# Layer 1's output projection, layer norm and ternary feed forward as one pipeline of four stages over token tiles

## The chip, the cores and the metric

The program runs on one core of one Trainium2 chip. The core has a matrix engine (TensorE, PE in the profile, with its weight loads shown apart as PEld), VectorE (DVE), ScalarE (ACT), GpSimd (POOL) and SyncE (SP), which here only issues DMAs. Each engine takes its instructions in the order in which they were laid down; engines wait for each other by semaphores. Matrix products land in PSUM, everything else lives in the on-chip memory SBUF or in the device memory behind the DMA queues. The metric is the device time of one execution in microseconds (us), lower being better.

## The reference, cut to what matters

The program is a decoder of four layers on x of 8 x 100 tokens and 512 features. Each layer adds a cross attention on a context of 8 x 361 rows and then a feed forward, both of a layer-normed x. The change concerns the end of layer 1's attention and all of its feed forward:

```python
# end of _L1_xattn_ref: ctx is the attention's result, 800 x 512
delta = _nan_clean(ctx @ Wo.T + bo)
rs = jnp.clip(residual_scale, 0.0, RES_SCALE_MAX)
delta = rs * delta
mu = delta.mean(axis=-1, keepdims=True)
var = jnp.mean((delta - mu) ** 2, axis=-1, keepdims=True)
delta = (delta - mu) / jnp.sqrt(var + EPS_LN) * ln_gamma + ln_beta
...
def activation_quant(x):       # per token, to 8 bits
    scale = 127.0 / jnp.clip(jnp.max(jnp.abs(x), axis=-1, keepdims=True), EPS, None)
    return jnp.clip(jnp.round(x * scale), -128.0, 127.0) / scale
def weight_quant(w):           # to -1, 0, 1 times the mean size
    scale = 1.0 / jnp.clip(jnp.mean(jnp.abs(w)), EPS, None)
    return jnp.clip(jnp.round(w * scale), -1.0, 1.0) / scale
...
x = x + _L1_xattn_ref(_layernorm(x), ctx_2048, ...)
x = x + _L1_ffn_ref(_layernorm(x), w1, w2)   # bitlinear(relu(bitlinear(x, w1)), w2)
```

w1 is 2048 x 512 and w2 is 512 x 2048. The straight-through terms of the reference (x + stop_gradient(xq - x)) leave the values as above.

## The kernel before, in words

x stays in SBUF as seven tiles of up to 128 tokens (`TILES`; the last has 32). The program is written against a tile framework: it lays down instructions per engine in an order that a scheduler chooses at compile time from what is ready, inserts all semaphores, and hands out memory from stacked pools. Only inside `in_order()` are TensorE's matmuls and transposes kept in written order. A pool reuses the memory of pools closed before it; by default its tiles wait until all of that memory has been released, and with `reuse_waits="tile"` each waits only for what lay under it.

The work around the change is laid out as follows.

- `top2_experts` (layer 0's feed forward, lines 878 to 1186) sends tokens through experts in pairs of blocks. Meanwhile POOL writes the routing table of the last layer by 16 chained scatters (L1990). At its end `follow()` (L1172) starts layer 1's prefetch: `load_context` and `clipped_begin`, which load biases, context, the four attention weights (`weights_of`) through SP, and compute batch 0's keys and values. Then the expert results are gathered back by POOL into "got" (L1179) and added to x by VectorE (L1186).
- `clipped_attention` (L1304) first makes queries (`project_q`: layer norm, transposes, products) and then runs through the eight batches. `weigh(b)` multiplies queries and keys, clips on VectorE (L1337) and takes exponentials on ScalarE (L1338), with the next batch's keys (L1221, ScalarE adds the bias) and values (L1227, VectorE adds the bias) as TensorE's filling. `gather(b)` sums rows, copies the sums (ScalarE, L1367), inverts them (VectorE, L1368 and L1369), multiplies weights and values and writes the result over the queries in qT (L1370). Each `weigh` also runs two `fillers`: the sums of |w1| and |w2|, their means, and the rounding of w1 in four parts.
- `Ternary.quantise` rounds a 128 x 2048 part of a weight: VectorE scales and bounds above (L1446), bounds below and adds the number MAGIC, which rounds (L1447), and ScalarE takes MAGIC off and writes bf16 (L1448). The part comes through `load_v`, which has two buffers.
- After the last batch `tail()` rounds w2's four parts. Then bo, gamma and beta are loaded, POOL scales bo by the residual scale (L1385) and adds beta to x (L1259). TensorE multiplies all seven tiles by Wo (f32, four products of 128 x 512 a tile); VectorE forms delta (L1393), its statistics in two groups of tiles (L186, L187, a square root on ScalarE, L190), and updates x (L1399, L1407).
- `quantised_ffn` takes the statistics of x for all seven tiles at once and then runs a pipeline of three stages over the tiles: `start` (normalise, L196; largest magnitude, L1478; scale and round on VectorE, L1483; to bf16 on ScalarE, L1484), `widen` (transposes, 16 bf16 products with w1, Relu on ScalarE in four pieces, L1519, then the same rounding on 2048 columns) and `narrow` (16 transposes, 16 products with w2, the add to x, L1531). TensorE's order is the scheduler's here.
- PSUM results of these stages share `ps1`, four buffers of one bank; copies out of PSUM alternate between VectorE (L83) and ScalarE (L85) through `evac`.
- `softmax_attention` of layer 2 follows, beginning with batch 0's keys and values, which do not depend on x.

Of the kernel before, what the change touches and what calls it, by code (L numbers as in the profile page):

```python
# [26 lines left out]
ALU = mybir.AluOpType  # L27
# [32 lines left out]
def decoder_kernel(ctx: ExitStack, tc: tile.TileContext, a: dict, out: bass.AP):  # L60
# [817 lines left out]
    def top2_experts(far_rows, aside, follow):  # L878
# [6 lines left out]
        with ExitStack() as st, in_order():  # L885
# [285 lines left out]
            out_to_x(hT, downs, TILES[4:])  # L1171
            follow()  # L1172
            hst.close()
# [99 lines left out]
    def clipped_begin(ctxT, loads, st):  # L1273
# [8 lines left out]
        bv = load_row(res, "a1_bv")  # L1282
# [4 lines left out]
        nc.vector.tensor_scalar(rs, rs, 0.0, 0.3, ALU.max, ALU.min)  # L1287

# [13 lines left out]
        return wq, wk, wv, wo, bqk, bv, rs, msc, mbi, kst, kvp, kv  # L1302

    def clipped_attention(ctxT, begun, st, fillers, tail):  # L1304

        root = HR
        wq, wk, wv, wo, bqk, bv, rs, msc, mbi, kst, kvp, kv = begun
# [3 lines left out]
        hp = hst.enter_context(tc.tile_pool(name="a1h", bufs=2))  # L1311

# [69 lines left out]
        tail()  # L1382
        with tc.tile_pool(name="a1d", bufs=1) as dp:
            bo, gamma, beta = (load_row(dp, n) for n in ("a1_bo", "a1_gamma", "a1_beta"))
            nc.gpsimd.tensor_scalar(bo, bo, rs, None, ALU.mult)  # L1385
            add_row_to_x(beta)
            delta = dp.tile([128, NTT, D], F32, name="delta")
            nc.gpsimd.memset(delta[:, NTT - 1, :], 0.0)
            for tiles in (TILES[:4], TILES[4:]):
                for t, rows in tiles:  # L1390
                    p = ps1()
                    mm(p[:rows, :], [(qT[:, k, t * 128 : t * 128 + rows], wo[:, k, :]) for k in range(KD)])
                    nc.vector.scalar_tensor_tensor(  # L1393
                        delta[:rows, t, :], p[:rows, :], rs[:rows, :], bo[:rows, :], ALU.mult, ALU.add
                    )
                t0 = tiles[0][0]
                mv, rstd = norm_stats(delta[:, t0 : t0 + len(tiles), :], len(tiles))
                for t, rows in tiles:
                    nc.vector.scalar_tensor_tensor(  # L1399
                        delta[:rows, t, :],  # L1400
                        delta[:rows, t, :],
                        mv[:rows, t - t0, 0:1],
                        gamma[:rows, :],
                        ALU.subtract,
                        ALU.mult,
                    )
                    nc.vector.scalar_tensor_tensor(  # L1407
                        x[:rows, t, :],
                        delta[:rows, t, :],
                        rstd[:rows, t - t0 : t - t0 + 1],  # L1410
                        x[:rows, t, :],
                        ALU.mult,
                        ALU.add,
                    )
# [3 lines left out]
    class Ternary:  # L1418
# [25 lines left out]
        def quantise(self, i):  # L1444
            w = load_v(self.src[i])
            nc.vector.tensor_scalar(w, w, self.inv, 1.0, ALU.mult, ALU.min)  # L1446
            nc.vector.tensor_scalar(w, w, -1.0, MAGIC, ALU.max, ALU.add)  # L1447
            nc.scalar.activation(self.q[:, i, :], w, AF.Identity, bias=unmagic)  # L1448

    unmagic = const.tile([128, 1], F32, name="unmagic")  # L1450
    nc.vector.memset(unmagic, -MAGIC)

    def first_block(ctxT, begun):

        with ExitStack() as st:
            w1 = Ternary(st.enter_context(tc.tile_pool(name="f1q", bufs=1)), "f1_w1")
            w2 = Ternary(None, "f1_w2")
            fillers = [lambda w=w, i=i: w.add_up(i, w1.q[:, i, :]) for w in (w1, w2) for i in range(4)]
            fillers += [w1.average, w2.average] + [lambda i=i: w1.quantise(i) for i in range(4)]

            def tail():
                w2.room(st.enter_context(tc.tile_pool(name="f1r", bufs=1)))
                for i in range(4):
                    w2.quantise(i)

            clipped_attention(ctxT, begun, st, fillers, tail)
            quantised_ffn(w1, w2)

    def quantised_ffn(w1, w2):
        NI = INTER // 128  # L1470
        q1, q2 = w1.q, w2.q.rearrange("p i (k n) -> p (i k) n", n=D)
        with tc.tile_pool(name="f1h", bufs=2) as hp:

            def quantise(dst, src, rows):
# [8 lines left out]
                nc.vector.tensor_scalar(src, src, s, MAGIC, ALU.mult, ALU.add)  # L1483
# [17 lines left out]
            stats = norm_stats(x, NTT)  # L1501

            def start(t):
                y = hp.tile([128, D], F32, name="y")
                normed(y, x, stats, t)
                yq = hp.tile([128, D], BF16, name="yq", bufs=3)
                step = quantise(yq, y, 128)
                nc.vector.tensor_tensor(step, step, w1.mean, ALU.mult)
                return yq, step
# [25 lines left out]
            for i in range(NTT + 2):  # L1535
                if i < NTT:
                    started[i] = start(i)
                if 0 <= i - 1 < NTT:
                    wide[i - 1] = widen(*TILES[i - 1], started.pop(i - 1))
                if 0 <= i - 2:  # L1540
                    narrow(*TILES[i - 2], wide.pop(i - 2))
# [772 lines left out]
```

## Time and profile before

| | us |
|---|---|
| median of three runs (2099.94, 2108.53, 2112.19) | 2108.53 |
| the profiled execution's own time | 2107.41 |
| its span, first to last instruction | 2105.6 |
| TensorE busy in it | 1906.6 (91%) |
| VectorE busy | 838.6 (40%) |
| ScalarE busy | 522.4 (25%) |
| GpSimd busy | 229.0 (11%) |

All times below are counted from the start of the span. L1's attention over the batches runs from 626 to 865, the output projection from 862 on, the feed forward from 905, and layer 2's first products begin at 986.8. In groups of instructions, a line names source line, engine, operation, output <- inputs and shapes, then count, busy time and mean duration, and last the idle time of the engine just before them with what ended it. A matmul that is issued in f32 shows as two passes. A helper's line (L102 for products, L107 for transposes, L83 and L85 for copies) stands for all its callers, so groups are told apart by the names of their tiles.

### The profile page before, as it was taken

How to read it: one execution, taken by the hardware profiler on the slowest of the kernel's cores; microseconds unless marked ns; L12 is line 12 of the kernel's file. 1: busy time of each engine (PE TensorE's matmuls, PEld its weight loads, DVE VectorE, ACT ScalarE, POOL GpSimd, SP SyncE). 2: the span in 40 equal slices, each digit the busy share in tenths (PEclk: the TensorE clock that was granted, in tenths of full speed). 3: DMA queues.
4: the chain of work that ended last, by engine and by line, in shares of the span. 5: the costliest groups of instructions: out<-in, count | busy, mean ns of one | idle time of the engine just before them, and what ended most of it. 6: DMA issues, size and time to landing. Idle time of an engine off the chain costs nothing.

```text
span 2105.6 us, 28969 instructions
## 1 busy us (share of the span) xinstructions
PE 1906.6 (91%) x12195; PEld 1123.6 (53%) x12202; DVE 838.6 (40%) x1579; ACT 522.4 (25%) x1149; POOL 229.0 (11%) x197
## 2 busy tenths in 40 slices
PE   6999999879879989758999999999998999979994
PEld 4576655423345545424555554555444555539994
DVE  6254444634253253875455555101112333331221
ACT  2243233124142232344244443000001111001110
POOL 4100000121210000200100000000002000024543
PEclk8999999989989999979999998999998999999997
DMA  8610000468960012300000001111002000026993
GB/s 220 214 47 31 31 21 2 195 210 258 333 217 1 1 47 75 116 1 11 21 1 1 1 24 38 40 40 60 20 30 57 15 1 2 21 81 206 251 263 65
DMA packets 61565, 171.99 MB, mean 82 GB/s; under 512 B 18840, under 2 KB 27332, under 8 KB 54640
## 3 DMA queue, kind: packets, MB, share of 16 engines
q1 hardware_dynamic: 35122, 135.37, 18.7%
q0 software_dynamic: 21296, 25.42, 5.3%
q10 hardware_dynamic: 5006, 9.22, 1.3%
q8 instruction: 100, 1.64, 0.3%
q14 instruction: 41, 0.34, 0.0%
HBM read 146.10 MB, written 19.55 MB: 79 GB/s over the span
## 4 chain that ended last, share of the span: by engine, by line
PE 46%; issue 12%; DVE 8%; DMA 3%; ACT 2%; POOL 1%; POOLq 0%; ACTq 0%; DVEq 0%; SPq 0%
PE ps L102 43%; PE ps L107 3%; DMA out_x<-o,r_row 2%; DVE rl L1369 1%; ACT sc L1582 1%; DVE va L1227 1%; DVE amax L1478 1%; DMA read<-table 1%; DVE y L196 1%; DVE sc L1587 0%; DVE nmx L1579 0%; DVE st L186 0%; DVE h L1483 0%; ACT hq L1484 0%; POOL out_x L2015 0%
## 5 line engine op out<-in xcount | busy, mean ns | idle before, releaser
L102 PE MATMUL ps<-w,ctxT 128*128 128x512 f32 (+1 forms) x576 | 267.5, 608 | 11.5 <-DVE va L1227 11.5
L102 PE MATMUL ps<-yT,w 128*128 128x400 f32 x800 | 274.6, 505 | 0.4 <-DMA w<-in_f_gu 0.4
L102 PE MATMUL ps<-ctxT,w 128*128 128x361 f32 x768 | 252.0, 475 | 9.6 <-DVE va L1227 9.6
L102 PEld LDWEIGHTS ps<-yT,w 128*128 128x128 f32 x800 | 152.6, 192 | 117.9 <-issue 5.2
L102 PEld LDWEIGHTS ps<-ctxT,w 128*128 128x128 f32 x768 | 142.0, 190 | 103.1 <-issue 19.8
L102 PEld LDWEIGHTS ps<-w,ctxT 128*128 128x128 f32 (+1 forms) x576 | 103.5, 186 | 132.1 <-issue 110.7
L1221 ACT ACTIVATE kT<-ps,bqk 128x361 f32<-128x361 f32 x96 | 53.7, 560 | 270.9 <-PE ps L102 269.7
L102 PE MATMUL ps<-xT,w 128*128 128x152 f32 (+1 forms) x768 | 105.4, 298 | 1.3 <-issue 0.7
L102 PEld LDWEIGHTS ps<-xT,w 128*128 128x128 f32 (+1 forms) x768 | 101.8, 185 | 2.7 <-issue 0.9
L102 PE MATMUL ps<-w_vo,oc 128*128 128x512 f32 (+1 forms) x224 | 91.3, 601 | 0.0
L227 DVE TENSOR_TENSOR x<-x,ps 128x512 f32<-128x512 f32 (+1 forms) x52 | 35.6, 685 | 138.3 <-PE ps L102 138.3
L1227 DVE TENSOR_TENSOR va<-ps,r_a_bv 128x512 f32<-128x512 f32 (+1 forms) x72 | 48.1, 682 | 102.1 <-PE ps L102 102.1
L874 DVE TENSOR_TENSOR hT<-sg,ps 128x400 f32<-128x400 f32 x36 | 20.4, 570 | 162.5 <-PE ps L102 162.5
L102 PE MATMUL ps<-w,qT 128*128 128x512 f32 (+1 forms) x176 | 79.3, 606 | 4.8 <-DVE qT L1821 4.8
L1582 ACT ACTIVATE sc<-ps,nmx 100x361 f32<-100x361 f32 x128 | 70.2, 561 | 50.2 <-DVE nmx L1579 50.1
L107 PEld LDWEIGHTS ps<-ident,sc 100*128 100x128 f32 (+1 forms) x512 | 54.3, 153 | 41.8 <-issue 28.5
L2097 POOL DMA_INDIRECT out_x<-o,r_row x32 | 59.0, 1844 | 96.8 <-DMA out_x<-o,r_row 41.5
L107 PE MATMUL ps<-ident,sc 100*128 100x100 f32 (+1 forms) x512 | 63.8, 262 | 5.7 <-DVE va L1227 3.9
L2001 POOL DMA_DIRECT2D read<-table x1 | 3.5, 3487 | 568.0 <-issue 568.0
L1338 ACT ACTIVATE pT<-pT,mbi,msc 128x800 f32<-128x800 f32 (+1 forms) x48 | 48.5, 1046 | 63.9 <-DVE pT L1337 63.9
L592 ACT ACTIVATE sc<-sc,nmx 100x128 f32<-100x128 f32 x128 | 49.8, 390 | 55.6 <-DVE nmx L589 53.8
L102 PE MATMUL ps<-w,xT 128*64 128x512 f32 x256 | 61.2, 622 | 0.8 <-DVE xT L83 0.8
(372 smaller groups left out, 2756.9 us busy)
## 6 DMA issues: line engine op xcount, KB each, us to landing
w<-in_f_gu SPq DMA_DIRECT2D x32, 704.0 KB, 6.7
wd<-in_f_dn SPq DMA_DIRECT2D x32, 512.0 KB, 4.8
v<-in_f_w SPq DMA_DIRECT2D x16, 1024.0 KB, 5.4
w<-in_a_w SPq DMA_DIRECT2D x12, 1024.0 KB, 6.9
v<-in_f_dn SPq DMA_DIRECT2D x16, 768.0 KB, 9.1
w<-in_f_gu SPq DMA_DIRECT2D x9, 1024.0 KB, 4.7
gu<-in_f_gu SPq DMA_DIRECT2D x8, 1024.0 KB, 18.0
cx<-in_ctxT SPq DMA_DIRECT2D x8, 722.0 KB, 7.6
```

What stands on the lines that cost most here:

```text
L102: ins = nc.tensor.matmul(dst, **args)
L107: ins = nc.tensor.transpose(dst, src, unit)
L196: nc.vector.tensor_scalar(dst, src[:, t, :], mv[:, t, 0:1], rstd[:, t : t + 1], ALU.subtract, ALU.mult)
L227: nc.vector.tensor_tensor(x[:rows, t, :], x[:rows, t, :], p[:rows, :], ALU.add)
L592: nc.scalar.activation(sc[:, g, :], sc[:, g, :], AF.Exp, bias=nmx[:, g : g + 1], accum_out=l[:, g : g + 1])
L1221: nc.scalar.activation(kT[:, m, :], p[:, :LK], AF.Identity, bias=bk[:, m : m + 1])
L1227: nc.vector.tensor_tensor(va[:kn, c, :, 0:HD], p[:kn, :].rearrange("p (h d) -> p h d", d=HD), bv[:kn, :].rearrange("p (h d) -> p h d", d=H ...
L1338: nc.scalar.activation(dst, dst, AF.Exp, bias=mbi[:kn, b, c : c + 1], scale=msc[:kn, b, c : c + 1])
L1369: nc.vector.reciprocal(rl, rl)
L1478: nc.vector.tensor_reduce(amax, src, AX.X, ALU.max, apply_absolute_value=True)
L1582: nc.scalar.activation(sc[:, h, :], s[i][:LQ, g, :LK], AF.Exp, bias=nmx[:, g : g + 1], accum_out=l[:, h : h + 1])
L2097: nc.gpsimd.indirect_dma_start(out=flat, out_offset=bass.IndirectOffsetOnAxis(ap=r_row[:, e, h : h + 1], axis=0), in_=o[:, h, :], in_offse ...
```

## The change

Six things are edited.

1. `follow()` is called after the experts' pool is closed, instead of before.
2. `clipped_begin` also loads the rows bo and gamma, and POOL scales bo there.
3. beta is loaded into a slot of the attention's `pT` buffers right after the queries, and POOL adds it to x then.
4. The rounding of a weight part is now two steps on ScalarE (scale and add MAGIC; take it off and write bf16) and one clamp to -1 .. 1 on VectorE, in bf16 and in place. In `quantise` of activations the scaling and rounding goes to ScalarE where the row is 512 wide; the 2048 wide one stays on VectorE.
5. The output projection, its norm, the x update and the statistics of x become a stage `attended`, one tile at a time, in front of `start`, `widen` and `narrow`. Iteration i runs `attended(i)`, rounds part i of w2 (i < 4), then `start(i - 1)`, `widen(i - 2)` and `narrow(i - 3)`.
6. The loop runs inside `in_order()`, so TensorE keeps the written order, and its pools reuse memory tile by tile.

```diff
             out_to_x(hT, downs, TILES[4:])
+            hst.close()
             follow()
-            hst.close()
...
-        bv = load_row(res, "a1_bv")
+        bv, bo, gamma = (load_row(res, n) for n in ("a1_bv", "a1_bo", "a1_gamma"))
...
         nc.vector.tensor_scalar(rs, rs, 0.0, 0.3, ALU.max, ALU.min)
+        nc.gpsimd.tensor_scalar(bo, bo, rs, None, ALU.mult)
...
         hp = hst.enter_context(tc.tile_pool(name="a1h", bufs=2))
+        beta = hp.tile([128, 4, KD * LQ], F32, name="pT", bufs=5)[:, 0:2, :].rearrange("p g q -> p (g q)")[:, :D]
+        nc.sync.dma_start(out=beta, in_=a["a1_beta"].partition_broadcast(128))
+        add_row_to_x(beta)
...
         def quantise(self, i):
-            w = load_v(self.src[i])
-            nc.vector.tensor_scalar(w, w, self.inv, 1.0, ALU.mult, ALU.min)
-            nc.vector.tensor_scalar(w, w, -1.0, MAGIC, ALU.max, ALU.add)
-            nc.scalar.activation(self.q[:, i, :], w, AF.Identity, bias=unmagic)
+            w, q = load_v(self.src[i]), self.q[:, i, :]
+            nc.scalar.activation(w, w, AF.Identity, bias=magic, scale=self.inv)
+            nc.scalar.activation(q, w, AF.Identity, bias=unmagic)
+            nc.vector.tensor_scalar(q, q, -1.0, 1.0, ALU.max, ALU.min)
...
+            qT = clipped_attention(ctxT, begun[1], st, fillers)
+            w2.room(st.enter_context(tc.tile_pool(name="f1r", bufs=1, reuse_waits="tile")))
+            with in_order():
+                quantised_ffn(qT, begun[0], w1, w2)
...
-                nc.vector.tensor_scalar(src, src, s, MAGIC, ALU.mult, ALU.add)
+                if src.shape[1] == D:
+                    nc.scalar.activation(src, src, AF.Identity, bias=magic[:rows, :], scale=s)
+                else:
+                    nc.vector.tensor_scalar(src, src, s, MAGIC, ALU.mult, ALU.add)
...
-            stats = norm_stats(x, NTT)
+            stats = [hp.tile([128, NTT, n], F32, name=f"s{i}", bufs=1) for i, n in enumerate((2, 1, 2, 1))]
+
+            def attended(t, rows):
+                mv, rstd, mvx, rstdx = (v[:, t, :] for v in stats)
+                p = ps1()
+                mm(p[:rows, :], [(qT[:, k, t * 128 : t * 128 + rows], wo[:, k, :]) for k in range(KD)])
+                d = hp.tile([128, D], F32, name="y", bufs=3)[:rows, :]
+                nc.vector.scalar_tensor_tensor(d, p[:rows, :], rs[:rows, :], bo[:rows, :], ALU.mult, ALU.add)
+                tile_stats(mv[:rows, :], rstd[:rows, :], d)
+                nc.vector.scalar_tensor_tensor(d, d, mv[:rows, 0:1], gamma[:rows, :], ALU.subtract, ALU.mult)
+                nc.vector.scalar_tensor_tensor(
+                    x[:rows, t, :], d, rstd[:rows, :], x[:rows, t, :], ALU.mult, ALU.add
+                )
+                tile_stats(mvx, rstdx, x[:, t, :])
...
-            for i in range(NTT + 2):
+            for i in range(NTT + 3):
                 if i < NTT:
-                    started[i] = start(i)
+                    attended(*TILES[i])
+                if i < 4:
+                    w2.quantise(i)
                 if 0 <= i - 1 < NTT:
-                    wide[i - 1] = widen(*TILES[i - 1], started.pop(i - 1))
+                    started[i - 1] = start(i - 1)
+                if 0 <= i - 2 < NTT:
+                    wide[i - 2] = widen(*TILES[i - 2], started.pop(i - 2))
+                if 0 <= i - 3:
+                    narrow(*TILES[i - 3], wide.pop(i - 3))
```

The removed block at the end of `clipped_attention` is the sequence told above (L1383 to L1414). `tile_stats` (L198) is the per-tile form of the statistics: VectorE's two statistics operations, a square root on ScalarE, a reciprocal on VectorE.

## The prediction

> **What bounds the kernel now.** I read the page's busy shares first: TensorE (PE) is busy 91% of 2105.6 us, so only a stretch in which PE stands still can be worth much. The busy time by stretches (columns: length, then busy time of PE, its weight loads, VectorE (DVE), ScalarE (ACT), GpSimd (POOL), then PE's granted clock and DMA) places it at the seam between L1's attention and its feed forward:
>
> ```profile
> 858.00:865.00 7.00, 7.00 (x112) 4.25 (x107) 4.17 (x4) 2.23 (x3) 0.00 (x0) 1.00 0.01 2
> 865.00:885.00 20.00, 20.00 (x48) 8.20 (x47) 14.20 (x16) 5.90 (x3) 13.68 (x9) 1.00 0.46 150
> 885.00:909.00 24.00, 1.17 (x7) 0.30 (x4) 23.50 (x62) 4.98 (x7) 1.86 (x1) 0.60 0.32 127
> 909.00:930.00 21.00, 14.94 (x73) 6.74 (x73) 13.27 (x34) 12.83 (x16) 0.00 (x0) 0.81 0.00 1
> 930.00:987.00 57.00, 45.66 (x284) 22.81 (x290) 38.45 (x91) 31.73 (x43) 0.00 (x0) 1.00 0.03 10
> ```
>
> From 865 to 885 PE multiplies by Wo without a pause; from 885 to 909 it does 1.2 us while DVE is full; until 930 its clock is 0.81. So the seam is bound by DVE first and PE only afterwards. The groups of that stretch (name, shape, count | busy, mean ns | idle before, releaser) give the prices:
>
> ```profile
> L102 PE MATMUL ps<-w,qT 128*128 128x512 f32 (+1 forms) x54 | 23.6, 594 | 0.0
> L1478 DVE TENSOR_REDUCE amax<-h 128x1 f32<-128x2048 f32 (+1 forms) x7 | 15.9, 2279 | 6.0 <-ACT h L1519 6.0
> L1484 ACT ACTIVATE hq<-h,unmagic 128x2048 bf16<-128x2048 f32 (+1 forms) x7 | 14.0, 2002 | 16.6 <-DVE step L1486 14.3 <-DVE ascale L1482 2.3
> L1399 DVE SCALAR_TENSOR_TENSOR delta<-delta,mv,r_a_gamma 128x512 f32<-128x512 f32 (+1 forms) x7 | 7.1, 1015 | 0.1
> L1407 DVE SCALAR_TENSOR_TENSOR x<-delta,rstd,x 128x512 f32<-128x512 f32 (+1 forms) x7 | 4.8, 738 | 0.0
> L1446 DVE TENSOR_SCALAR v<-v,inv_f_w 128x2048 f32<-128x2048 f32 x2 | 4.0, 1986 | 0.0
> L107 PE MATMUL ps<-identb,yq 128*128 128x128 bf16 (+1 forms) x28 | 2.8, 225 | 22.8 <-ACT yq L1484 22.8
> ```
>
> The last one is the stall itself: 22.8 us until tile 0's rounded yq. The timeline in order shows what went before, and where PE leaves for L2's keys:
>
> ```profile
> 864.59 0.57 DVE L1370 TENSOR_TENSOR qT<-ps,rl 128x400 f32<-128x400 f32 x1
> 870.90 0.75 DVE L1393 SCALAR_TENSOR_TENSOR delta<-ps,rs,r_a_bo 128x512 f32<-128x512 f32 x1 [5.73 <-POOL r_a_bo L1385]
> 904.68 1.00 DVE L196 TENSOR_SCALAR y<-x,mv,rstd 128x512 f32<-128x512 f32 x2
> 908.70 0.61 PE L107 MATMUL ps<-identb,yq 128*128 128x128 bf16 x4 [22.83 <-ACT yq L1484]
> 910.38 4.95 PE L102 MATMUL ps<-q_f_w,yqT 128*128 128x512 bf16 x15 [1.08 <-ACT yqT L85]
> 986.77 2.70 PE L102 MATMUL ps<-ctxT,w 128*128 128x361 f32 x8
> ```
>
> DVE waits 5.73 us for bo (loaded, then scaled on POOL), then norms all seven tiles before the first y. The seam runs from 862.3 (unbroken Wo matmuls) to 986.8, 124.5 us. PE needs at full clock: Wo 28 x 0.857 (two passes of 0.43 us) = 24.0; per tile yq transposes 0.39, widening 3.63, hq transposes 1.06, narrowing 3.63 = 8.71, times 7 = 61. So 85, and 39.5 us are lost.
>
> **The change part by part.**
>
> *1. The pipeline's start.* Only tiles 5 and 6 need the last batch, so the bound is Wo on tile 0 (862.3 + 3.43 = 865.7) and DVE's release by L1370 at 865.2. Then tile 0 alone: delta 0.73, statistics 0.68 + 0.17, root on ACT 0.30, reciprocal 0.16, x update 0.74 (gamma's runs beside the root), statistics of x again 1.31, y 0.54, amax 0.68, three small operations at 0.18 = 0.54, two ACT steps at 0.71 = 1.42, transposes 0.39, copy 0.5: 8.2 us, so 873.9. Tile 1's own 4.2 us of DVE can come between: 878.1. I take the middle, 876, against 910.4 before. PE meanwhile has Wo of tiles 0 to 2 until 872.6; it idles about 3.5 us, and I add 1 us for a lower clock afterwards (0 to 3: the first 16 widening matmuls took 4.95 us at 15 recorded where 3.63 is the warm figure, and one narrowing took 4.47).
>
> *2. Iterations 3 to 6.* Each holds Wo 3.43, a widening 4.02, a narrowing 4.69: PE 12.14 us. DVE per tile: attended 4.2, start 2.0 (y's scaling, 0.48, goes to ACT), widen 4.3 (amax 2.28, scaling 1.28, five small), narrowing's add 0.73, half of the copies 0.9: 12.1 by rows. Neighbours overlap (two L196 of 0.54 take 1.00), about 0.08 us over some 20, so 10.5 in fact. ACT: roots 0.6, yq 1.4, four Relu 2.75, hq 2.0, copies 1.3: 8.0. PE stays the longest. In the loop of before a tile took 9.57 us (L1531 from 929.53 to 986.88, six steps) where PE's work is 8.71, 1.10 times; so 12.14 x 1.10 = 13.3, four of them 53.
>
> *3. The end.* Two iterations without Wo at 9.57 = 19.1; the last tile 6.8, as before (979.97 to 986.77). First widening 3.6. The sum: 876 + 3.6 + 53 + 19.1 + 6.8 = 958.8, with the clock 959.8. At the start DVE has a backlog: attended 0 to 3 (16.8), start 0 to 2 (6) and widen 0 (4.3) come to 27, with overlap 24, from 865.7 to 890, plus hq 2.0, while PE wants to narrow tile 0 at 888: 3 us more (0 to 5). The end is 963, and 24 us are saved. Bounds: DVE's busy time from 865 to 987 is 89.4 us; without y's scaling (3.3), L1446 and L1447 (7.3), and gamma's slowed part (2), with four clamps (at most 4.9, by L1447's 1.23 for equal size), 81 remains: DVE could be through at 946, and hq, transposes and the last narrowing end near 953, a gain of 34. At 15 us an iteration and a start at 880 the end is 974, a gain of 13.
>
> *4. w2's rounding.* Per part ACT does two steps of 2.0 (L1448's row) instead of one, DVE one clamp instead of 1.27 + 1.22. Four parts in iterations 0 to 3 put ACT at 12 us an iteration: hidden under 13.3, exposed if ACT already waits (up to 4). Counted in the backlog above. The clamp in bf16 has no row; from above 1.23, from below next to nothing.
>
> [...]
>
> *5. w1's rounding, inside attention.* The batch that holds it took 35.0 us (row-sum matmuls at 770.84, 805.86) where its neighbours take 31.65: 3.4 us are paid now, because DVE's values add stands behind L1446 and L1447. That goes; in its place ACT's copy of the row sums, L1367, on which PE's next products wait (0.61 us now), can stand behind four roundings: 770.4 + 8.0 = 778.4 instead of 773.1, 5.3 us late. From -3.4 to +5.3; +1 as the middle.
>
> *6. bo and gamma loaded early, bo scaled on POOL.* The SP queue gets two row loads (0.43 us each to issue, 256 KB) ahead of the context's. POOL is waiting 4.8 to 5.8 us between table scatters (L1990), and the gathers "got" that PE waits for (11.5 us) are behind them. In such a gap the 1.57 us cost nothing; ahead of a scatter, with bo landing near 546 against 544.87, up to 2.7, and the bytes up to 1.3. I take 0: gaps are the larger part. In return the 5.73 us of the seam are gone (counted in 1).
>
> *7. beta in a pT slot, added by POOL as attention begins.* 13.45 us of POOL; beside it DVE was slower (gamma's 1.55 against 0.74; L1446 2.29 against 1.27). In 640 to 680 DVE has 9.57 of 40 us, so at worst 13.45 x 0.24 doubled, +3.2; at best nothing, since what the seam gains by the adds' leaving is in items 1 to 3. PE's 38 of 40 is its cover: 0. The slot is wanted again for batch 1, after 655; the adds end near 645. beta's DMA waits on SP for project_q's yT (626); behind it is one weight load for L2, needed much later.
>
> *8. Closing the expert pool before the prefetch* issues nothing. From 0 to +2, should the prefetched values fall on a late tile; 0, as these are first written after 626.
>
> Sum: -24 + 1 = -23. The profiled execution took 2107.41 (span 2105.6, 1.8 around it), 1.1 under the median of 2108.53: 2107.41 - 23 = 2084.4, said against the median 2085.
>
> **The rivals.**
>
> *A smaller gain: ACT takes DVE's place.* Iterations 0 to 3 at 12 us of ACT plus waits run 15 each instead of 13.3, hq comes late, and item 5 goes its bad way: +5 and +4, with item 6 at +2.7: 2096. For it: ACT runs in order, and a 2 us rounding can stand ahead of a 0.3 us root. Against it: ACT's idle share of 44% in the loop.
>
> *It does not overlap.* DVE's 81 us exist in either order; if PE and DVE keep alternating as in 885 to 909, 16.5 us an iteration (4 x 3.2 more) leaves some 10 us: 2097. For it: DVE would be 81 of 98 us. Against it: tiles t, t-1, t-2 and t-3 are independent.
>
> *Slower: PE's written order against DVE's queue.* PE may not pass Wo(i) by; its result keeps one of the four PSUM buffers ps1 until DVE reads it, which stands behind another tile's amax and scaling, while widen needs four such buffers and a transpose one. If each Wo(i) then waits for the earlier tile's whole DVE turn, an iteration is 12.1 + 10.5 = 22.6 us and the seam ends at 963 + 4 x 9.3 = 1000: 2122. It decides from 19.3 us an iteration, where the gain of 24 is gone. Against it: in the loop of before PE's waits for all copies come to some 20 us in 78 with the same four buffers.
>
> **How the numbers follow.** Forecast 0.62 (its own range 2073 to 2094), ACT 0.14, no overlap 0.13, slower 0.11. About 0.5%, 10.5 us, is what a measurement tells from nothing, so 2098 and 2119 are the marks. The smaller-gain cases lie around 2097 and give half of the no-overlap case and a part of ACT's to "same". Faster 0.77, same 0.12, slower 0.11. The range takes the bounds of items 1 to 7 (-34 - 3.4 below: 2070; +11, +4.3, +2.7, +3 above: near 2105) and leaves out the slower case and the tails: 2068 to 2105.
>
> **What will show it.** In the trace after, the first widening matmul starts between 874 and 880, no PE idle over 5 us follows in the seam, PE's clock in its stretch is 0.95 or more, gamma's update takes 0.74, L2's keys begin near 963 (all shifted by what items 5 to 7 move attention's end). The batch with w1's rounding lasts 31.6 to 38. The prediction is wrong if the iterations take over 16 us, if row sums of that batch wait on ACT, or if "got" comes later than 577.

## The result and the profile after

The changed kernel takes 2111.29 us (median of 20 runs), the kernel before 2111.11 us (20 runs beside it): a ratio of 1.0002, 95% interval 0.9988 to 1.0015. Nothing was gained; the forecast of 2085 us was 26 us too low. The profiled execution after took 2110.94 us, with a span of 2109.2.

TensorE's share is 91% as before. The busy time of the seam by stretches, after (columns: from:to, length, then busy time of PE, its weight loads, VectorE, ScalarE, GpSimd, PE's granted clock, DMA share, GB/s), cut at the first Wo product, the first widening, Wo of tile 3, the end of tile 3's narrowing and L2's keys:

```profile
867.18:887.50 20.32, 11.18 (x31) 4.83 (x29) 19.08 (x45) 16.36 (x16) 0.00 (x0) 0.87 0.49 179
887.50:893.37 5.87, 5.87 (x16) 2.28 (x17) 0.33 (x2) 3.59 (x6) 0.00 (x0) 0.58 0.24 99
893.37:956.03 62.66, 51.62 (x242) 23.13 (x241) 46.77 (x110) 31.51 (x45) 0.00 (x0) 0.92 0.05 18
956.03:989.57 33.54, 24.64 (x138) 10.88 (x136) 18.04 (x46) 15.72 (x22) 0.00 (x0) 0.90 0.05 16
```

At the start TensorE still waits beside a busy VectorE (19.1 of 20.3 us), for 8.5 us where it was 22.8. What is new is spread out: from 893 on no engine is full, and yet PE is idle for 11.0 and 8.9 us, and no stretch has the clock at 1.00. The waits of PE over the whole seam, 867 to 990, after (waiting stage, releaser, total us, times, longest):

```profile
PE ps L107 <- ACT yq L1460: 8.5, 1, 8.5
PE ps L102 <- DVE yqT L83: 5.4, 2, 2.7
PE ps L102 <- ACT s L203: 4.2, 1, 4.2
PE ps L102 <- ACT yqT L85: 3.3, 3, 1.9
PE ps L102 <- ACT hqT L85: 2.7, 3, 1.1
PE ps L107 <- ACT hq L1460: 2.5, 1, 2.5
```

With the smaller ones they come to 29 us where they were 40 before, but PE's busy time in the seam rose from 84.2 to 93.3 us. Most of that is the clock: the 14 widenings and narrowings, the same products, took 52.9 us before and 61.2 after. (About 1 us more is two Wo products that ran ahead of the seam before.) PE's timeline after shows it (start, duration, line, operation, count, wait before):

```profile
867.18 10.57 PE L102 MATMUL ps<-w,qT 128*128 128x512 f32 x24
886.21 0.61 PE L107 MATMUL ps<-identb,yq 128*128 128x128 bf16 x4 [8.46 <-ACT yq L1460]
887.50 6.04 PE L102 MATMUL ps<-q_f_w,yqT 128*128 128x512 bf16 x16 [0.68 <-DVE step L1462]
893.37 3.60 PE L102 MATMUL ps<-w,qT 128*128 128x512 f32 x8
896.81 0.39 PE L107 MATMUL ps<-identb,yq 128*128 128x128 bf16 x4
901.36 5.94 PE L102 MATMUL ps<-q_f_w,yqT 128*128 128x512 bf16 x16 [4.17 <-ACT s L203]
...
932.09 5.31 PE L102 MATMUL ps<-q_f_w,yqT 128*128 128x512 bf16 x16 [2.66 <-DVE yqT L83]
...
959.16 3.63 PE L102 MATMUL ps<-q_f_w,yqT 128*128 128x512 bf16 x16 [2.75 <-DVE yqT L83]
...
970.81 5.31 PE L102 MATMUL ps<-q_f_w,yqT 128*32 128x512 bf16 x16 [1.92 <-ACT yqT L85]
...
984.33 5.31 PE L102 MATMUL ps<-q_f_w,hqT 128*32 128x512 bf16 x16 [0.18 <-DVE hqT L83]
989.57 2.70 PE L102 MATMUL ps<-ctxT,w 128*128 128x361 f32 x8
```

A widening costs 3.63 us with a warm clock, that is at a granted clock of 1.00; behind four of the five waits of 1.9 us or more it costs 5.31 to 6.04, at a granted clock of 0.58 to 0.68. The first Wo product starts 4.9 us later than before (862.3), L2's keys 2.8 us later (986.8). So the whole gain of the seam is 2.1 us (124.5 to 122.4), and something ahead of it has lost 4.9.

The wait of 4.17 us is named after a square root on ScalarE, but the widening needs yqT. VectorE's timeline after shows where that copy stood:

```profile
894.29 2.29 DVE L1451 TENSOR_REDUCE amax<-h 128x1 f32<-128x2048 f32 x1 [6.46 <-ACT h L1509]
...
897.19 1.29 DVE L1459 TENSOR_SCALAR h<-h,ascale 128x2048 f32<-128x2048 f32 x1
...
898.46 0.73 DVE L1485 SCALAR_TENSOR_TENSOR y<-ps,rs,r_a_bo 128x512 f32<-128x512 f32 x1
...
899.18 0.54 DVE L196 TENSOR_SCALAR y<-x,s,s 128x512 f32<-128x512 f32 x1
899.63 0.69 DVE L201 BATCH_NORM_STATS2 st<-y 128x6 f32<-128x512 f32 x1
900.24 0.67 DVE L1451 TENSOR_REDUCE amax<-y 128x1 f32<-128x512 f32 x1
...
900.91 0.39 DVE L83 COPY yqT<-ps 128x512 bf16<-128x512 bf16 x1
```

VectorE first stood idle for 6.46 us until the Relu of tile 0's h. Then a copy of 0.39 us, whose input was ready at 897.2, waited behind the scaling of h and seven shorter operations, all of them other tiles', until 900.9, and PE started within 0.1 us of its end. Both engines waited in turn for each other, although the tiles are independent.

Ahead of the seam, GpSimd's timeline after and then before, around the last table scatter:

```profile
571.96 0.97 POOL L1984 DMA_INDIRECT table<-said,at_i  x1 [4.95 <-DMA table<-said,at_i]
572.97 1.58 POOL L1288 TENSOR_SCALAR r_a_bo<-r_a_bo,rs 128x512 f32<-128x512 f32 x1
574.73 1.03 POOL L1179 DMA_INDIRECT got<-back,where_i  x1 [0.18 <-issue]
```

```profile
569.48 0.97 POOL L1990 DMA_INDIRECT table<-said,at_i  x1 [4.79 <-DMA table<-said,at_i]
570.75 1.00 POOL L1179 DMA_INDIRECT got<-back,where_i  x1 [0.30 <-DMA ctxT<-in_ctxT]
```

The scaling of bo lies exactly between the last scatter and the first gather. From the last scatter to attention's first product it takes 60.4 us after, 56.7 before. (The last scatter itself, 2.5 us later here, came anywhere from 568.9 to 576.6 in the executions of this study.) Inside attention 1.7 us come back: the batch of row sums that holds w1's rounding lasts 33.3 us instead of 35.0.

### The profile page after: what moved, and what is told of

Read it like the earlier page. It is cut to its first block, busy times and chain, and to the rows that moved or that the text cites. A ratio compares the mean times of both kernels' runs of the same rounds, so it can differ in the third digit from the quotient of the medians.

```text
span 2109.2 us, 28986 instructions
## 1 busy us (share of the span) xinstructions
PE 1916.2 (91%) x12202; PEld 1126.7 (53%) x12202; DVE 818.0 (39%) x1573; ACT 545.8 (26%) x1175; POOL 223.6 (11%) x196
## 4 chain that ended last, share of the span: by engine, by line
PE 46%; issue 13%; DVE 7%; DMA 6%; ACT 3%; POOL 1%; POOLq 0%; ACTq 0%; DVEq 0%
PE ps L102 43%; PE ps L107 3%; DMA table<-said,at_i 2%; DMA out_x<-o,r_row 2%; ACT sc L1576 1%; DVE va L1227 1%; DVE rl L1373 1%; DVE amax L1451 1%; DVE y L196 1%; DMA read<-table 1%; DVE st L201 1%; ACT v L1418 0%; DVE sc L1581 0%; POOL got L1179 0%; DVE nmx L1573 0%
## 5 line engine op out<-in xcount | busy, mean ns | idle before, releaser
L2091 POOL DMA_INDIRECT out_x<-o,r_row x32 | 58.9, 1841 | 97.5 <-DMA out_x<-o,r_row 39.9
L1342 ACT ACTIVATE pT<-pT,mbi,msc 128x800 f32<-128x800 f32 (+1 forms) x48 | 48.6, 1046 | 59.7 <-DVE pT L1341 59.7
L873 ACT ACTIVATE sg<-ps 128x400 f32<-128x400 f32 x36 | 18.1, 504 | 171.2 <-PE ps L102 171.2
```

Source lines behind the costliest of these rows:

```text
L1342: nc.scalar.activation(dst, dst, AF.Exp, bias=mbi[:kn, b, c : c + 1], scale=msc[:kn, b, c : c + 1])
L2091: nc.gpsimd.indirect_dma_start(out=flat, out_offset=bass.IndirectOffsetOnAxis(ap=r_row[:, e, h : h + 1], axis=0), in_=o[:, h, :], in_offse ...
```

## The experiments

Medians of these kernels, taken in separate runs, are certain to 0.2 to 0.4%, some 6 us. The ratios with their 95% intervals come from all runs, so they differ a little from the quotient of two medians. The seam is read much more finely: from the last batch's row sums to L2's keys it took 149.3 us before and 147.6 after, and 147.0 to 147.7 in the three other executions below that left the seam's code alone. So each experiment is judged by that stretch first, called the seam's length here, and by its ratio to the kernel before second. The length splits into time in which PE is idle and time in which it is busy; the products are the same in all kernels. Of the 9.5 us of busy time between before and after, 8.3 are in the 14 widenings and narrowings (52.9 and 61.2), where 16 matmuls took 3.63 us at a granted clock of 1.00 and 5.31 at 0.68. So busy time is read as the clock's first; a little of it is records that a trace lacks (869 of PE's in the stretch before, 877 after):

| kernel | length, us | PE idle | PE busy |
|---|---|---|---|
| before | 149.3 | 44.1 | 105.1 |
| after | 147.6 | 33.0 | 114.6 |
| e1, e2, e8 (seam's code as after) | 147.0 to 147.7 | 33.0 to 33.7 | 113.3 to 114.7 |
| e3 | 145.2 | 33.7 | 111.6 |
| e4 | 147.8 | 35.0 | 112.8 |
| e5 | 143.0 | 32.6 | 110.4 |
| d1 | 144.5 | 32.4 | 112.1 |
| e6 | 148.0 | 36.4 | 111.6 |
| e7 | 140.3 | 29.3 | 111.1 |
| f2 | 135.8 | 23.5 | 112.3 |
| f3 | 134.3 | 22.6 | 111.7 |
| f4 | 133.1 | 21.0 | 112.1 |

Four of these rows in the profile (before, after, e5, f4; columns as above):

```profile
837.51:986.77 149.26, 105.12 (x869) 53.28 (x877) 109.39 (x218) 64.81 (x78) 15.55 (x9) 0.91 0.15 52
841.98:989.57 147.59, 114.59 (x877) 56.03 (x877) 101.68 (x219) 76.55 (x98) 0.00 (x0) 0.90 0.13 47
841.15:984.13 142.98, 110.43 (x869) 54.36 (x877) 101.88 (x219) 76.38 (x98) 0.00 (x0) 0.92 0.13 49
838.96:972.04 133.08, 112.06 (x877) 54.90 (x877) 104.46 (x223) 72.86 (x94) 0.00 (x0) 0.92 0.15 52
```

The order of the work moves the idle time, from 33.0 down to 21.0 us. The busy time differs by some 4 us between the pipelined kernels without following the waits, and in all of them it stays 5 us or more above the kernel before.

**Is the prefetch's loss the scaling of bo?** Two edits to the changed kernel: the scaling written later, as attention begins, and the same with the two row loads moved there too.

```diff
# e1_scale_late
-        nc.gpsimd.tensor_scalar(bo, bo, rs, None, ALU.mult)      # clipped_begin
+        nc.gpsimd.tensor_scalar(bo, bo, rs, None, ALU.mult)      # behind add_row_to_x(beta)
# e2_rows_late: as well
-        bv, bo, gamma = (load_row(res, n) for n in ("a1_bv", "a1_bo", "a1_gamma"))
+        bv = load_row(res, "a1_bv")
+        # bo, gamma: tiles here, loaded behind beta
```

> The changed kernel, with the rows bo and gamma still loaded early, but bo scaled on GpSimd only after the expert results were gathered and beta was added. Theory 'POOL's queue': the scaling at 572.97 (1.58 us) stands between the last table scatter and the first gather, so without it the first gather issues about 1.7 us earlier and attention begins near 630.5 instead of 632.3; the scatters stay at about 6.3 us each. Rival 'bytes': the two rows (512 KB) are what slowed the scatters and the gathers, and attention begins at 632 as before. Whole time: 0 to 2 us less than the changed kernel.

> The changed kernel with the rows bo and gamma loaded only after the queries (behind beta's) and bo scaled there. If the prefetch item as a whole costs what the traces differ by, attention begins again near 626 (626.15 in the kernel before, 632.3 in the changed one), 4 to 6 us less in the whole time. If the scatters and gathers merely vary from execution to execution, or another edit (closing the expert pool earlier) delays the stage, attention begins at 630 or later.

e1: ratio 1.0009 (0.9982 to 1.0036), e2: 0.9968 (0.9935 to 1.0001). In e1 the scheduler still laid the scaling between scatter and gather (575.87, 1.58 us), so e1 tested nothing. In e2 the first gather follows its scatter at once (574.10, 575.36), and attention starts 58.7 us after the last scatter instead of 60.4. With the scaling there, attention starts 59.9 to 61.0 us after the last scatter in eight executions of this study and 58.5 in a ninth (d1); without it (e2, e8, f3, f4), 58.6 to 59.0. So the position costs some 1.5 us, which by the medians can't be told from nothing, and no run brought back the 56.7 of the kernel before.

**Which copies wait, and is it enough to move them?** In e3 all copies of transposes go to ScalarE; in e4 tile i - 2's yq is transposed and copied before Wo of tile i.

```diff
# e3_copies_act
-                    evac(dst[:, k0 : k0 + n, :], p[...])
+                    nc.scalar.copy(dst[:, k0 : k0 + n, :], p[...])
# e4_turn_first
+                if 0 <= i - 2 < NTT:
+                    flat_y = turned(*TILES[i - 2], started.pop(i - 2))   # transposes and copy, out of widen
                 if i < NTT:
                     attended(*TILES[i])
```

> The changed kernel with all copies of the transposed yq and hq on ScalarE, none on VectorE. Theory 'order of the queues': TensorE waits not for VectorE's sum of work but for short copies that stand behind long operations in VectorE's order (4.2 + 2.7 + 2.7 us, each followed by a slow clock); the seam from 867.2 to 989.6 (122.4 us) shrinks by 8 to 14 us. Rival 'VectorE's throughput': only the copies' own 6 us of VectorE leave, TensorE waits elsewhere, and the seam shrinks by 0 to 4 us. Rival 'ScalarE': the copies queue behind 2 us roundings and it grows.

> The changed kernel with the transposes of yq(i-2) written ahead of Wo(i) instead of behind it, so that the copy has Wo's 3.4 us for itself. Theory 'order of the queues': the waits for yqT in iterations with Wo (4.2 and 2.7 us, and 0.7 in the others) go, with the slow clock behind them: 6 to 10 us less in the seam. Rival 'VectorE's throughput': no more than 2 us less. If yq is late itself, TensorE now waits ahead of Wo, and nothing is gained.

e3: 1.0002 (0.9977 to 1.0028), seam 145.2. e4: 0.9971 (0.9943 to 0.9999), seam 147.8; the low time of its profiled execution (2097.3 us) lies behind the seam (L2's keys to the end took 1107 us, 1120 in the kernel after). Neither gave the 8 to 14 or 6 to 10 us that the order of the queues had been expected to give; e3's 2.4 us even lie in the range of the rival, VectorE's throughput. Of the three waits that e3's expectation sees followed by a slow clock (4.2, 2.7 and 2.7 us), the last was followed by one of 1.00 (959.16 in the kernel after). The waits only moved: PE's idle time is no shorter in either. e3's, in the table of PE's waits:

```profile
PE ps L102 <- ACT hqT L1475: 10.8, 7, 3.1
PE ps L107 <- ACT yq L1460: 8.5, 1, 8.5
PE ps L102 <- ACT yqT L1475: 7.8, 6, 3.3
```

With no copy on VectorE, the copies now stand behind ScalarE's rounding of 2.0 us and its Relus of 0.68 us. In e4 hqT took over (12.0 us in all), and yq of tile 0, now ahead of Wo of tile 2, waited 11.1 us.

**Is it TensorE's written order, or VectorE's load?** e5 leaves TensorE's order to the scheduler. d1 leaves out part of the work: it takes the maximum of h over 512 of its 2048 columns, 1.6 us less for VectorE in each tile. It was timed once, at 2112.71 us, so only its trace is read.

```diff
# e5_nopin
-            with in_order():
-                quantised_ffn(qT, begun[0], w1, w2)
+            quantised_ffn(qT, begun[0], w1, w2)
# d1_quarter_amax
-                nc.vector.tensor_reduce(amax, src, AX.X, ALU.max, apply_absolute_value=True)
+                nc.vector.tensor_reduce(amax, src[:, :D], AX.X, ALU.max, apply_absolute_value=True)
```

> The changed kernel with the pipeline outside in_order(), so that the scheduler chooses TensorE's order too, as it did before. Theory 'the written order holds TensorE up': Wo(3) to Wo(6) move into the waits (8.5 us before the first yq), and the seam from the last full row sums to L2's keys (147.6 us in the changed kernel, 149.3 before) shrinks by 8 us or more. Theory 'the chain from h over VectorE and ScalarE to hq and back sets the pace': within 3 us either way.

> Leaves part of the computation out: the largest magnitude of h is taken over the first 512 of its 2048 columns, so the reduction falls from 2.29 to 0.68 us a tile, on VectorE and in the chain from h to hq alike. Theory 'VectorE's chain sets the pace': 1.6 us less for each of the seven tiles and the clock behind it, 147.6 falls by 9 to 15 us. Theory 'handoffs in the queues': under 5 us.

e5: 0.9973 (0.9944 to 1.0002), seam 143.0, 4.6 us shorter than after and between the two expected ranges; the same long waits (yq 8.5, yqT 5.4, s 4.2) stay. The written order costs next to no waiting (PE idle for 32.6 us, 33.0 after): 4.2 of the 4.6 us are PE's busy time, so the same products ran at a warmer clock (0.92 granted, 0.90 after). Why the clock was warmer is not shown. d1: seam 144.5. Taking 11 us from VectorE gives 3, of which 0.6 is waiting. Of its groups (count | busy, mean ns | idle before and releaser), two show why:

```profile
L1451 DVE TENSOR_REDUCE amax<-h 128x1 f32<-128x512 f32 x6 | 4.1, 686 | 3.6 <-ACT h L1509 3.5
L1521 DVE SCALAR_TENSOR_TENSOR x<-ps,step,x 128x512 f32<-128x512 f32 x6 | 4.5, 751 | 18.9 <-PE ps L102 18.9
```

VectorE gets the time and idles most of it away: from the first Wo product to L2's keys it is idle for 46.4 us in d1, 38.2 after, and 18.9 of them now lie ahead of the x updates, waiting for PE. The seam is not bound by how much VectorE has to do.

**The start, and the order of all three engines.** e7 only writes `start(i - 1)` ahead of `attended(i)` and of w2's rounding, so that tile 0's normalisation is not behind that work. f2 also transposes yq before Wo from iteration 3 on, puts hq's transposes ahead of the last quarter of the widening, so that copies run under matmuls, and fixes the yqT copy on VectorE and the two hqT copies on one engine each.

```diff
# e7_start_first
+                if 0 <= i - 1 < NTT:
+                    started[i - 1] = start(i - 1)
                 if i < NTT:
                     attended(*TILES[i])
...
# f2_spread: as well, in widen
                 for n in range(4):
+                    if n == 3:
+                        aside()          # transposes and copies of tile i - 3's hq
...
# and in the loop
+                if 2 < i < NTT + 2:
+                    turn = turned(*TILES[i - 2], started.pop(i - 2))
```

> The changed kernel with start(i-1) written ahead of attended(i) and of w2's rounding, so that VectorE's order favours the tile that is further on; TensorE's written order is the same. The first widening begins 20.3 us after the first Wo now (887.5 against 867.2). Theory 'tile 0 is interleaved with tiles 1 and 2': it begins 3 to 6 us sooner after Wo, and the whole seam is 3 to 8 us shorter. Theory 'what is gained at the start is lost in the loop, whose pace VectorE sets': the first widening sooner, the seam within 2 us.

> All of TensorE's short dependent steps get other products to hide behind: yq is transposed ahead of Wo (from the third tile on), hq's transposes stand before the last quarter of the widening, start is written ahead of attended. Theory 'handoffs in the queues': the waits for copies (13 us for yqT, 4.4 for hqT) and some of the 8.5 us at the start go, with the slow clock behind them; 147.6 falls by 15 to 22 us and the whole time to some 2092. Theory 'VectorE's chain sets the pace': TensorE waits for yq and hq themselves, 147.6 falls by under 6 us.

e7: 0.9971 (0.9946 to 0.9996), seam 140.3; the first widening came 17.4 us after the first Wo product, not 20.3. f2: 0.9940 (0.9917 to 0.9963), seam 135.8: 11.8 us from the order of the same operations, on the same engines but for the few copies. That is less than the 15 to 22 expected and twice what the rival allowed; 9.5 of it are waiting.

**The rounding on ScalarE.** e6 gives the weights their old rounding.

```diff
# e6_old_round
-            nc.scalar.activation(w, w, AF.Identity, bias=magic, scale=self.inv)
-            nc.scalar.activation(q, w, AF.Identity, bias=unmagic)
-            nc.vector.tensor_scalar(q, q, -1.0, 1.0, ALU.max, ALU.min)
+            nc.vector.tensor_scalar(w, w, self.inv, 1.0, ALU.mult, ALU.min)
+            nc.vector.tensor_scalar(w, w, -1.0, MAGIC, ALU.max, ALU.add)
+            nc.scalar.activation(q, w, AF.Identity, bias=unmagic)
```

> The changed kernel with the weights' rounding as before: two VectorE operations and one ScalarE step for a part of w1 and w2. If the new rounding is what shortens the batch of row sums that holds it (33.3 us against 35.0), the batch goes back to about 35 us. In the seam, where VectorE works off a backlog in the first three iterations, four parts put 4 x (2.5 - 0.67) = 7.3 us more on VectorE and take 8 us from ScalarE: if VectorE's backlog sets the seam, it lengthens by 3 to 7 us (147.6 to 151 to 155); if the waits are ScalarE's (yq behind roundings of 2 us), it shortens by 1 to 4. Time within 0.3% of the changed kernel either way.

e6: 1.0009 (0.9983 to 1.0034). The batch with w1's rounding went back to 35.0 us (its row sums at 778.4, the next at 813.4), so the 1.7 us there are the rounding's. The seam took 148.0, outside both expected shifts: at the start the old operations stood in VectorE's queue, the new ones in ScalarE's, and the first widening came 20.2 us after the first Wo product in e6 and 20.3 in the kernel after. The equal lengths hide two differences, though: PE is idle for 36.4 us in e6 against 33.0, and busy for 111.6 against 114.6. So the old rounding makes PE wait 3.4 us longer, and a warmer clock, whose cause is not shown, pays that back (0.90 granted from the first Wo product to L2's keys against 0.89; 58.9 us for the 14 widenings and narrowings against 61.2).

**The prefetch put back, and everything together.** e8 loads bo and gamma into attention's own pool as it begins, scales bo there, and closes the experts' pool behind the prefetch. f3 is f2 with that. f4 also transposes the next tile's yq as soon as a widening ends, in the iterations from 6 on, ahead of the maximum and the scaling of h in VectorE's order.

```diff
# e8_prefetch_back
-            hst.close()
             follow()
+            hst.close()
...
+        bo, gamma = (load_row(res, n) for n in ("a1_bo", "a1_gamma"))
         add_row_to_x(beta)
+        nc.gpsimd.tensor_scalar(bo, bo, rs, None, ALU.mult)
# f4_spread_ahead: f2 and e8, and in widen, behind the four pieces
+                ahead()                   # from i = 6: turn = turned(*TILES[i - 1], ...)
                 hq = hp.tile([128, INTER], BF16, name="hq")
                 step = quantise(hq, h, rows)
```

> The changed kernel with its prefetch as before: bo and gamma are loaded only as attention begins (behind project_q's weights on the queue, into attention's own pool), bo is scaled there by GpSimd, and the expert pool closes behind the prefetch. The seam is untouched. If the early rows and the scaling between the gathers cost what the profiles showed, attention begins 56.5 to 58 us after the last table scatter (60.4 in the changed kernel, 56.7 before) and the time falls by 3 to 5 us, to a ratio of 0.998; last row sums to L2's keys stay at 146 to 149 us. If the later start of attention was only a late chain of scatters in that execution, the 60 stays and so does the time.

> The seam spread (yq transposed ahead of Wo, hq's transposes ahead of the last quarter of the widening, short copies fixed to engines, start written first) together with the prefetch as before. If the two losses are separate, they add: last row sums to L2's keys about 136 us, attention 56.5 to 58 us after the last scatter, ratio 0.992. If the prefetch cost nothing, the ratio stays at the 0.994 of the spread alone.

> As the spread with the old prefetch, and in the iterations without Wo the next tile's yq is transposed and copied as soon as the widening ends, so that this copy of 0.3 us stands ahead of VectorE's maximum and scaling of h (3.5 us) and not behind them. If short copies behind long operations in VectorE's order are what is left, the waits of 2.8 and 1.9 us for yqT in the last iterations go, and with the warmer clock last row sums to L2's keys falls from 136 to 130 to 133 us. If yq itself is not ready by then, TensorE waits for it with the narrowing uncovered and nothing is gained: 135 to 138.

e8: 0.9965 (0.9937 to 0.9992), attention 58.9 us after the last scatter and so not at the expected 56.5 to 58, seam 147.0. Beside the kernel before, its trace accounts for some 2 us of gain in these stretches; the rest of the 7 in the ratio lies elsewhere or in the noise. f3: 0.9929 (0.9902 to 0.9956), seam 134.3. f4: 0.9893 (0.9856 to 0.9930), a median of 2091.32 beside 2112.49 for the kernel before; it beats both kernels. Its stretches up to L2's keys account for some 16 us, which the interval (15 to 30 us) includes. PE's waits and busy time in f4's seam:

```profile
PE ps L107 <- ACT yq L1461: 6.5, 2, 4.3
PE ps L107 <- ACT hq L1461: 4.3, 2, 3.4
PE ps L107 <- DVE st L201: 2.7, 1, 2.7
PE ps L102 <- ACT hqT L1476: 2.1, 5, 0.6
PE ps L102 <- DVE yqT L1476: 0.8, 1, 0.8
```

```profile
864.09:972.04 107.95, 90.84 (x424) 40.27 (x421) 87.08 (x205) 63.49 (x83) 0.00 (x0) 0.92 0.16 54
```

From the last row sums it took 133.1 us, just outside the expected 130 to 133; of the 14.5 us below the kernel after, 12.0 are waiting and 2.5 are PE's busy time. The waits for yqT fell from 4.7 in f2 to 0.8, as expected; a wait of 2.7 us came in their place. The profile names it after a statistics operation, but what ended then (946.0) is ScalarE's rounding of hq: the scaling of h ahead of it began at 942.4, behind a y, a maximum and an x update of other tiles, although its own maximum was done at 940.5. VectorE is busy 87 us in f4, 84 after: it never had to become lighter. From Wo to Wo, three iterations took 16.4 us on average in the kernel after and some 13 already in f2. In PE's timeline of f4 they take 14.0, 13.3 and 12.1 us, 13.1 on average, where the forecast had 13.3:

```profile
889.16 5.35 PE L102 MATMUL ps<-w,qT 128*128 128x512 f32 x8
...
903.16 3.65 PE L102 MATMUL ps<-w,qT 128*128 128x512 f32 x8
...
916.43 3.65 PE L102 MATMUL ps<-w,qT 128*128 128x512 f32 x8
...
928.55 3.62 PE L102 MATMUL ps<-w,qT 128*32 128x512 f32 x8
```

## Why the prediction was wrong

The forecast against the measurement, in the profiled executions: the seam ended 21.7 us later than forecast (989.6, where the forecast's 963 moved by the later first Wo product makes 967.9), attention ended 3.9 us later than the forecast's +1, and the stretch behind the seam took 0.8 more. Together 26.4 of the 26.5 us between 2084.4 and 2110.9. Two steps of the forecast failed in the seam. It scaled the waits of the old loop with PE's work ("1.10 times") and took the middle of two bounds at the start, where what decided was the order in which short operations stood in VectorE's and ScalarE's queues. And it gave a lower clock 1 us, where the 14 widenings and narrowings took 61.2 us, 10.3 more than at 3.63 each. The items below add up to 22.2 us and not 21.7, because the forecast's own terms, 962.5 together, were rounded up to 963.

*Item 1, the pipeline's start: too small by 6.6 us.* Counted from the later first Wo product, the forecast's 876 becomes 880.9, and it was 887.5. "I take the middle" failed: I let one other tile's work come between. VectorE took parts of tiles 1 and 2 and three clamps of w2 before tile 0's scale was ready (883.1), and ScalarE then finished a weight rounding (until 884.6) before it scaled y:

```profile
882.99 0.14 DVE L1455 TENSOR_SCALAR ascale<-ascale 128x1 f32<-128x1 f32 x1
882.71 1.99 ACT L1419 ACTIVATE q_f_w<-v,unmagic 128x2048 bf16<-128x2048 f32 x1
884.61 0.80 ACT L1457 ACTIVATE y<-y,magic,ascale 128x512 f32<-128x512 f32 x1
```

e7 recovers 2.9 us by writing `start` ahead of both.

*The first widening* took 5.9 us where 3.6 and 1 for the clock were allowed: 1.3 more.

*Item 2, the iterations: too small by 6.7 us*, and this is the wrong idea behind the forecast. Iterations 3 to 6 took 62.7 us, 15.7 each, where 53 and 3 of backlog stood; 3.1 us of the difference are PE's busy time (51.6 where 4 x 12.14 make 48.6), the rest waits. "1.10 times" carried the waits of the loop before over as a proportion of PE's work. But the waits here were no proportion of the work: from Wo to Wo the same work took 16.4 us in the kernel after and 13.1 in f4. What PE waited for was a short copy or a step that stood behind long operations of another tile in an engine's order (4.17 us for a copy of 0.39), and the new stage adds nine operations a tile for it to stand behind. By busy times everything fitted (VectorE 46.8 of 62.7 us), as the forecast had it. d1 shows that VectorE's load is not the cause, e3 that another engine for the copies isn't the cure, f2 and f4 that the order is: their iterations have the forecast's length. (The forecast also read "some 20 us in 78" of waits for copies in the loop before; the copies' waits there were 10.9 us, all waits 17.4.)

*Item 3, the end: too small by 7.6 us.* 25.9 stood, 33.5 were measured. The kernel before took 27.7 for the same products (959.1 to 986.8), so the average of 9.57 a tile was 1.8 too small for this end of the loop. Of the other 5.8, 2.0 are waiting (8.9 us against 6.8) and 3.8 PE's busy time: two groups of 16 matmuls took 5.31 instead of 3.63, a third 3.92. The forecast took these durations from a loop whose clock was 1.00; it was 0.90 here. The forecast's mark for the clock, 0.95 or more, fell.

*Item 4, w2's rounding hidden: right against the old rounding, not shown in itself.* e6 (148.0 against 147.6, and 3.4 us more waiting with the old operations) shows that the new ones are no worse. But at the start three clamps and a ScalarE step stood ahead of tile 0's scale and scaling (item 1), and no run leaves the rounding out.

*Item 5, w1's rounding: the right bounds, the wrong side of the middle.* -1.7 us instead of +1. Both effects were there: VectorE's delay went (e6 brings it back), and PE's wait for ScalarE's copy of the row sums grew from 0.6 to 1.8 us, not to 5.

*Item 6, bo early at no cost: wrong by 1.5 us.* "Gaps are the larger part" failed: the scaling landed in the one place behind the last scatter where no gap is. Another 1.8 us are in project_q, whose 64 products took 23.6 us instead of 21.8 at a granted clock of 0.92 instead of 1.00. e8, with the old prefetch, has 23.2 and 0.94, so the early rows are not the cause; what is the cause stays open.

*Items 7 and 8 at zero: right* as far as it can be told. From attention's first product to its last row sums it took 209.7 us after and 211.4 before, and the difference is item 5. The gamma update takes 0.74 us, as forecast. For item 8, e2 closes the experts' pool ahead of the prefetch and e8 behind it, both with the rows late, and attention starts 58.7 and 58.9 us after the last scatter.

*The rivals.* "It does not overlap", with 16.5 us an iteration, came nearest by the iteration, with 15.7; its picture of PE and VectorE in turn is what the timeline at 887 to 901 shows, while its price held for only four iterations, so its 2097 us were 14 too low. The slower rival's 2122 were 11 too high. That rival put the right mechanism (an in-order queue ahead of a copy) in the wrong place: the longest wait in an iteration was 4.2 us, never a whole turn of VectorE. "ACT takes DVE's place" is not borne out for the weights: e6 takes their rounding off ScalarE again, and PE waits longer. Scaling y stayed on ScalarE in every run, so that part was not tested.

What e5 showed in passing: with the same long waits and nearly the same idle time (32.6 us against 33.0), the same products took 4.2 us less at a granted clock of 0.92 against 0.90. So a colder clock cost time of its own here beside the waits, and removing waits did not bring all of it back: with 12.0 us less idle time, f4 still has 112.1 us of busy time where the kernel before had 105.1. No run set the clock on purpose, and what decides it stays open.

## What to carry to other kernels

This pipeline over independent tiles gained only as much as its in-order queues let through (from the last row sums to L2's keys 147.6 us in the order as first written, 133.1 in f4's, for the same operations). So for every short operation that the bound engine waits for, list what stands ahead of it on its own engine in the written order, and put it ahead of the long operations or its wait under other matmuls. Busy shares said nothing against waits (in iterations 3 to 6 ScalarE was busy 50% and VectorE 75% of the time, and PE waited 11.0 of 62.7 us); check the longest wait per iteration instead. When waits of 2 to 4.2 us remain, give the matmuls behind them a range: here 16 of them took from 3.63 us (behind 2.75) to 5.94 (behind 4.17), and behind the same wait of 2.66 us not the same in every kernel (3.63 to 5.31).

## What the runs showed of the hardware that was not expected

In these traces the clock does not follow from the wait just ahead. After a wait of 2.75 us the 16 widening matmuls at 959.16 took 3.63 us, after one of 1.92 us those at 970.81 took 5.31, and the last narrowing 5.31 after waits of 2.50 and 0.18. In the kernel before, the same narrowing behind the same two waits took 3.63:

```profile
982.47 0.56 PE L107 MATMUL ps<-identb,hq 32*128 32x32 bf16 x16 [2.50 <-ACT hq L1484]
983.21 3.63 PE L102 MATMUL ps<-q_f_w,hqT 128*32 128x512 bf16 x16 [0.18 <-DVE hqT L83]
```

And the widening behind the wait of 2.66 us, which took 5.31 at 932.09, took 5.31 in e2, 5.11 in d1 and 3.63 in e1, e5, e6 and e8. The granted clock in these stretches after:

```profile
959.16:962.79 3.63, 3.63 (x19) 1.74 (x20) 1.67 (x10) 3.63 (x7) 0.00 (x0) 1.00 0.00 0
970.81:976.12 5.31, 5.31 (x18) 1.97 (x18) 0.16 (x1) 2.17 (x4) 0.00 (x0) 0.68 0.00 0
984.33:989.57 5.24, 5.24 (x17) 1.90 (x17) 0.00 (x0) 0.22 (x1) 0.00 (x0) 0.67 0.00 0
```

So in one execution waits of 2.66 and 2.75 us were followed by a granted clock of 0.68 (932.09 to 937.40) and of 1.00, and a wait of 1.92 by 0.68. No run shows what decides between them.

The other surprise is where the kernel's spread lies: from L2's keys to the end, code that no edit touched, executions took 1107 to 1126 us. That alone is 0.9% of the time, and it hides gains of the size that single reorderings bring.
